# A graph layer's gathers partly replaced by copies of columns: 12 and 14 more columns a step

## The chip, the cores and the metric

The kernel runs on one core of a Trainium2 chip. The metric is the device time of one execution in microseconds. Engines are named PE (TensorE), DVE (VectorE), ACT (ScalarE), POOL (GpSimd) and SP (SyncE, which here issues most transfers).

## The reference

One message-passing layer over a graph of N = 12500 nodes with 64 features and E = 200000 edges, sorted by destination:

```
nodes = x[edges].reshape(E, 128)                      # source row, destination row
gates = (ssp(edge_state @ We1 + be1) @ We2 + be2) * soft_cutoff(distance)
h     = ssp(nodes @ Wn1 + bn1) @ Wn2 + bn2            # ssp(z) = softplus(z) - log 2
sums  = zeros_like(x).at[dst].add(h * gates)
x     = layernorm(x + x + ssp(sums @ Ws1 + bs1) @ Ws2 + bs2)
```

## The kernel before

The edges are cut into 391 groups of 512. A group is four columns (`k` = 0 to 3) of 128 edges. The main loop runs over steps `i`, one group a step, software-pipelined by hand: the program's order on each engine is the order in which the loop writes it (`tc.manual_schedule`).

The source rows of a group reach the chip by four indirect transfers, one for each column, which POOL issues (`gather`, L204); the four of a group follow each other and are called a burst here. They land in `xg`, a tile `[128 edges, 4, 128]` with eight buffers. Its first 64 entries are the source row, the next 42 a one-hot row that says which of 42 neighbouring nodes the edge ends in (`onehot`, L277). TensorE transposes the four columns (`transposes`, L283), ScalarE copies the result out of PSUM (`xcopy`, tile `xT`, L291), and the first layer multiplies it (`layer1_node`, L308) with weights whose lower rows are the destination nodes' own products, read from a table in HBM (SP, `wns`). ScalarE takes exponential and logarithm (`exps` L322, `logs` L325), VectorE finishes the softplus (L330). The second layer (`layer2`, L354 and L359) gives gates and `h`; VectorE multiplies them (`hcut` L368, `message` L372). `scatter` (L376) multiplies the messages with the one-hot rows, and `window` (L396) adds the result to `sums`. Matmuls called `busy` (L334) fill TensorE's idle time.

In step `i` TensorE's order is: the biases, `scatter(i-2)`, `transposes(i+1)`, the edge part of layer 1, a `busy` matmul or, early on, the table's next chunk (`chunk`, L646), `layer1_node(i+1)`, a `busy` matmul, `layer2(i)`. A gather of group `g` reuses the `xg` buffer of group `g-8` and so waits for `scatter(g-8)`.

Every so often a block of 512 nodes has all its edges, and its final part is worked in pieces over the next steps (`node_block`): two of the pieces have matmuls (`hidden` L415, `layer2` L443 and L446), and the others are VectorE's and ScalarE's (L425 to L475).

Some columns of edges are not gathered. Half of x lies transposed on the chip (`xh`, 128 partitions by 6250 columns of 4 bytes; nodes from 6250 on are in the upper 64 partitions). `columns(i, queue, pool)` copies single columns of `xh`, at addresses read into registers, into a tile `column` of 128 columns (L259); queue 0 is VectorE, 8 copies a step, and queue 1 is ScalarE, 16 a step, from step 8 on. `read_columns` loads the addresses into the engine's registers (L242). When 128 columns are whole, `choose` (L271) clears for each edge the half that isn't its node, with the help of a tile `side` that SP loads. The result enters `layer1_node` as one more matmul (L311), and the column of `xg` is set to zero instead of being gathered (L202). Which column of which group this is, a slot, is fixed ahead by `slots_by_columns`: a slot is placed as soon as enough columns have been copied, and never in two adjacent groups. In a step the copies of ScalarE stand behind `xcopy`, and the ones of VectorE behind the softplus and the one-hot rows:

```
xcopy(i + 1)
columns(i, 1, finish)
...
at(onehot, i + 3)
read_columns(i, 0)
columns(i, 0, finish)
choose(finish)
```

Of the kernel before, what the change touches and what calls it, by code (L numbers as in the profile page):

```python
# [12 lines left out]
U8 = mybir.dt.uint8  # L13
# [12 lines left out]
P = 128  # L26
# [8 lines left out]
AHEAD = 3  # L35
# [5 lines left out]
BEHIND = 5  # L41
# [2 lines left out]

BLOCK_STEPS = ((2, 3, 4, 4, 6, 7, 8, 9, 10, 14), (2, 3, 3, 4, 5, 6, 7, 8, 9, 10), (1, 2, 1, 2, 3))
COLUMNS = (8, 16)
BASES = 4
COLUMNS_FROM = 8
XH_PARTS = 4
# [21 lines left out]
    return steps  # L71


def slots_by_columns(NG):

    slots, taken = [], set()
    for queue in (1, 0):
        columns, n = COLUMNS[queue], 0
        for g in range(NG - 2):
            if (g - 3 - COLUMNS_FROM + 1) * columns >= (n + 1) * P and not {g - 1, g, g + 1} & taken:  # L80
                slots.append((queue, g, queue + 1))
                taken.add(g)
                n += 1
    return sorted(slots)


def column_columns(NG):

    queues = [queue for queue, _, _ in slots_by_columns(NG)]
    return [-(-queues.count(queue) // columns) * columns if columns else 0 for queue, columns in enumerate(COLUMNS)]  # L90


def chunk_of(i, NCH):
# [11 lines left out]
def gnn_resnorm_kernel(ctx: ExitStack, tc: tile.TileContext, a: dict, out: bass.AP, E: int):  # L105
    nc = tc.nc
    x = a["x"]
    N = x.shape[0]
    NG = a["eT"].shape[1]
# [55 lines left out]
    be3 = const.tile([PIECES, 2, D], BF16, name="be3")  # L165
    row3 = const.tile([PIECES, 2, K, D], BF16, name="row3")
    rs3 = const.tile([PIECES, K, D], BF16, name="rs3")
    slots = slots_by_columns(NG)
    by_columns = {(g, k) for _, g, k in slots}
    columns_of = column_columns(NG)  # L170
    columns_at = const.tile([P, sum(columns_of)], I32, name="columns_at")
# [56 lines left out]
    engines = ((nc.vector, DVE), (nc.scalar, ACT))  # L228
    own = [[slot for slot in slots if slot[0] == queue] for queue in range(2)]
    column_tiles, side_tiles, chosen_columns = {}, {}, {}  # L230
    column_at, columns_done, whole = [[], []], [0, 0], []

    def columns_left(i, queue):
        return len(own[queue]) * P - columns_done[queue] if i >= COLUMNS_FROM else 0

    def read_columns(i, queue):

        if columns_left(i, queue) <= 0:
            return
        n, count = columns_done[queue], COLUMNS[queue]  # L240
        p, q = (n // count) % P, queue * columns_of[0] + n // (count * P) * count
        column_at[queue] = nc.values_load_multi_w_load_instructions(  # L242
            columns_at[p : p + 1, q : q + count], engines=[engines[queue][1]], min_val=xh_at,
            max_val=xh_at + 4 * (half_n - 1), skip_runtime_bounds_check_because="src holds rows of x")[1]

    def columns(i, queue, pool):

        count = min(COLUMNS[queue], columns_left(i, queue))
        for j in range(count):
            m, r = divmod(columns_done[queue] + j, P)  # L250
            slot = own[queue][m]
            if r == 0:
                column_tiles[slot] = pool.tile([P, P], F32, name=f"column{queue}", bufs=2)
                side_tiles[slot] = pool.tile([P, P], I32, name=f"side{queue}", bufs=2)
                at = slots.index(slot)
                nc.sync.dma_start(side_tiles[slot], a["sides"][at : at + 1, :].rearrange("o p -> (o p)")
                                  .partition_broadcast(P))
            copy = nc.vector.tensor_copy if queue == 0 else nc.scalar.copy
            copy(column_tiles[slot].bitcast(U8)[:, 4 * r : 4 * r + 4], xh[:, bass.ds(column_at[queue][j] - xh_at, 4)])  # L259
            if r == P - 1:  # L260
                whole.append(slot)
        columns_done[queue] += max(count, 0)

    def choose(pool):

        while whole:
            queue, g, k = slot = whole.pop(0)
            chosen_columns[g, k] = pool.tile([P, P], F32, name=f"chosen{queue}", bufs=2)
            for h, op in enumerate((OP.is_lt, OP.is_ge)):
                part = slice(h * D, (h + 1) * D)  # L270
                nc.vector.scalar_tensor_tensor(chosen_columns[g, k][part], side_tiles[slot][part], float(half_n),  # L271
                                               column_tiles[slot][part], op, OP.mult)
# [51 lines left out]
    def logs(g, part=every):  # L324
        nc.scalar.activation(us[g][:, part], us[g][:, part], AF.Ln, bias=one)  # L325
# [160 lines left out]
    with tc.manual_schedule():  # L486
# [50 lines left out]
        def clear(first, last):  # L537
            nc.vector.memset(sums[:, first * P : WIDE if last == NCH else last * P], 0.0)
# [43 lines left out]
        for i, w in enumerate((we2[:D, 0, :], wn2)):  # L582
            n = w.shape[0]
# [83 lines left out]
        with tc.tile_pool(name="finish", bufs=1) as finish:  # L667
# [4 lines left out]
            def at(f, g, *more):  # L672
                if 0 <= g < NG:
                    f(g, *more)
# [13 lines left out]
            for i in range(-1, last - 1):  # L688
                now = parts.pop(i, [])
                early = [part for part in now if part.tensor]  # L690
                at(load, i + LOADS)
                if i >= 0:
                    at(gather, i + AHEAD, range(K), [("transposes", i)] if i < BEHIND else ())
                layer1_bias(i + 1)
                at(layer2_bias, i)
                for n, g in enumerate(behind_by(i)):
                    scatter(g, zs[i + 1][:, 1, HE + 2 * n * W : HE + 2 * (n + 1) * W])
                transposes(i + 1, ("load", i + 1), ("gather", i + 1), ("onehot", i + 1))
                xcopy(i + 1)
                columns(i, 1, finish)  # L700
                layer1_edge(i + 1)
                c = chunk_of(i, NCH)
                if c is None:
                    busy_before_node(i + 1)
                else:
                    beside_sums = zs[i + 1][:, 1, HE + 2 * W : HE + 2 * W + P]
                    chunk(c, beside_sums)
                layer1_node(i + 1)
                exps(i + 1)
                logs(i + 1)  # L710
                if c is not None:
                    keep_chunk(c, beside_sums)
                read_columns(i + 1, 1)
                for g in behind_by(i):
                    window(g)
                if c is not None:
                    clear(c, c + 1)
                at(busy_before_layer2, i)
                at(layer2, i)
                for part in early:  # L720
                    part.tensor(tx_tile())
                at(hcut, i)
                at(message, i)
                softplus(i + 1)
                for part in early:
                    part.others()
                at(onehot, i + 3)
                read_columns(i, 0)
                columns(i, 0, finish)
                choose(finish)  # L730
                for part in now:
                    if not part.tensor:
                        part.others()
                for action in beside.get(i, []):
                    action()
# [134 lines left out]
def layouts(inputs):  # L870
# [8 lines left out]
    NG = -(-E // GE)  # L879
# [3 lines left out]
    def padded(v, n, fill):  # L883
        return np.concatenate([v, np.full((n - v.shape[0],) + v.shape[1:], fill, v.dtype)])
# [8 lines left out]
    slots = slots_by_columns(NG)  # L893
    out["sides"] = np.ascontiguousarray(np.stack([src_slots[:, g, k] for _, g, k in slots]))
    parts = []
    for queue, (count, n) in enumerate(zip(COLUMNS, column_columns(NG))):
        if n:
            v = np.concatenate([src_slots[:, g, k] for q, g, k in slots if q == queue])
            parts.append(padded(v, P * n, 0).reshape(-1, P, count).transpose(1, 0, 2).reshape(P, n))
# [52 lines left out]
```

## Time and profile before

| | us |
|---|---|
| median of 3 runs | 2363.53 (2359.99 to 2370.90) |
| the profiled execution | 2389.88 |
| its span, first to last instruction | 2388.1 |
| PE busy | 1970.5 (83%) |
| PE weight load busy | 1656.7 (69%) |
| ACT busy | 1511.2 (63%) |
| POOL busy | 1417.0 (59%), 1493 gathers |
| DVE busy | 1293.9 (54%) |

A line of the timeline reads: start in us from the start of the span, duration in us, engine, line of the kernel, operation, tile written and tiles read, shapes, how many such instructions are merged, and in brackets the engine's idle time before it and what ended that. A line of the waits reads: engine, tile and line that waited, for what; total in us, how often, the longest. A line such as `L242 ACTq TENSOR_LOAD ... x2: a/b/c, s to t` gives shortest, median and longest duration in ns and the start of the first and the last in us; a q behind the engine says that its sequencer runs it.

### The profile page before, as it was taken

The numbers are of one execution on the slowest core, as the hardware profiler recorded it, in microseconds if no ns is written. First come the engines' busy times: TensorE is split into PE (matmuls) and PEld (weight loads), VectorE is DVE, ScalarE is ACT, GpSimd is POOL, SyncE is SP. The second block draws the span as 40 slices with busy tenths as digits, with TensorE's granted clock in tenths as the row PEclk, the third lists the DMA queues.
The fourth block names the chain that finished last, engine by engine and source line by source line (L and its number), as shares of the span: only waits on it lengthen the run. The fifth ranks groups of instructions, "written<-read, shape, count | busy, mean of one in ns | idle before, by whom it ended". The sixth has DMA issues, their size and how long they took to land.

```text
span 2388.1 us, 48209 instructions
## 1 busy us (share of the span) xinstructions
PE 1970.5 (83%) x12897; PEld 1656.7 (69%) x12897; DVE 1293.9 (54%) x5966; ACT 1511.2 (63%) x7412; POOL 1417.0 (59%) x1497
## 2 busy tenths in 40 slices
PE   6788888888888888888888888888888888888877
PEld 4666677767776776677677667766777767777765
DVE  4355555555555555555555555555555555555544
ACT  3466666666666666666666666666666666666653
POOL 5665665666666666666666666665665666666650
PEclk9799999999999999999999999999999999999988
DMA  6332232322222222222222222222222222222220
GB/s 185 85 91 68 56 75 56 77 61 71 54 57 56 53 59 54 57 56 62 53 59 55 57 58 55 59 59 54 58 58 56 59 57 60 63 57 58 59 50 14
DMA packets 159679, 148.63 MB, mean 62 GB/s; under 512 B 40564, under 2 KB 108949, under 8 KB 159274
## 3 DMA queue, kind: packets, MB, share of 16 engines
q1 hardware_dynamic: 111194, 94.97, 14.4%
q0 software_dynamic: 47776, 49.02, 10.8%
q8 instruction: 109, 1.79, 0.3%
q14 instruction: 166, 1.36, 0.2%
q10 hardware_dynamic: 434, 1.50, 0.2%
HBM read 135.70 MB, written 9.62 MB: 61 GB/s over the span
## 4 chain that ended last, share of the span: by engine, by line
PE 80%; issue 13%; ACT 3%; DVE 2%; another core or an unknown queue 1%; DMA 0%; DVEq 0%; ACTq 0%
PE z L308 18%; PE gh L359 13%; PE z L376 10%; PE tx L283 10%; PE gh L354 7%; PE z L301 6%; PE gh L334 4%; PE gh L347 3%; PE z L296 3%; PE z L334 2%; ACT xT L291 2%; PE tx L415 1%; PE tx L446 1%; PE z L311 1%
## 5 line engine op out<-in xcount | busy, mean ns | idle before, releaser
L204 POOL DMA_INDIRECT xg<-in_x,src_i x1493 | 1416.8, 949 | 919.3 <-PE tx L283 488.8
L308 PE MATMUL z<-xT,wns 106*128 106x256 f32 x1564 | 459.7, 412 | 359.9 <-issue 285.9
L291 ACT COPY xT<-tx 106x512 f32<-106x512 f32 x391 | 229.1, 586 | 779.3 <-PE tx L283 751.1
L259 ACT COPY column<-xh 128x4 uint8 x6016 | 608.7, 193 | 0.0
L308 PEld LDWEIGHTS z<-xT,wns 106*128 106x128 f32 x1564 | 267.8, 193 | 452.4 <-issue 337.7
L368 DVE TENSOR_TENSOR h<-gh,cut 128x256 f32<-128x256 f32 x391 | 165.9, 424 | 747.9 <-PE tx L283 632.2
L359 PE MATMUL gh<-consts,s 128*128 128x64 f32 x3128 | 396.0, 270 | 0.0
L359 PEld LDWEIGHTS gh<-consts,s 128*128 128x128 f32 x3128 | 385.0, 194 | 0.1
L325 ACT ACTIVATE u<-u,one 128x768 f32<-128x768 f32 x392 | 365.8, 933 | 13.4 <-ACT u L322 0.5
L330 DVE SCALAR_TENSOR_TENSOR s<-u,z 128x768 f32<-128x768 f32 x392 | 368.7, 941 | 0.4 <-issue 0.4
L322 ACT ACTIVATE u<-z 128x768 f32<-128x768 f32 x392 | 314.7, 803 | 43.4 <-PE z L308 19.0
L396 DVE TENSOR_TENSOR sums<-sums,z 64x42 f32 x778 | 152.4, 196 | 291.3 <-issue 207.4
L376 PEld LDWEIGHTS z<-xg,msg 128*128 128x128 f32 x1556 | 205.0, 192 | 140.6 <-issue 121.3
L376 PE MATMUL z<-xg,msg 128*128 128x84 f32 x1556 | 265.1, 293 | 15.3 <-DVE msg L372 15.3
L259 DVE COPY column<-xh 128x4 uint8 x2944 | 246.5, 219 | 0.4 <-issue 0.4
L354 PE MATMUL gh<-consts,s 128*128 128x128 f32 x1564 | 243.3, 279 | 1.3 <-DVE s L330 0.8
L283 PE MATMUL tx<-consts,xg 128*106 128x128 f32 x1564 | 238.1, 276 | 0.0
L301 PE MATMUL z<-eT,consts 128*128 128x256 f32 x782 | 237.3, 386 | 0.0
L354 PEld LDWEIGHTS gh<-consts,s 128*128 128x128 f32 x1564 | 210.0, 195 | 2.0 <-DVE s L330 1.1
L283 PEld LDWEIGHTS tx<-consts,xg 128*106 128x106 f32 x1564 | 182.5, 142 | 0.9 <-issue 0.9
L372 DVE TENSOR_TENSOR msg<-gh,h 128x256 f32<-128x256 f32 x391 | 165.8, 424 | 13.4
L334 PEld LDWEIGHTS gh<-consts 128*128 128x128 f32 x778 | 149.5, 195 | 20.5 <-issue 0.3
(109 smaller groups left out, 1456.2 us busy)
## 6 DMA issues: line engine op xcount, KB each, us to landing
eT<-in_eT SPq DMA_DIRECT2D x195, 256.0 KB
xg<-in_x,src_i POOLq DMA_INDIRECT x1493
wns<-table SPq DMA_DIRECT2D x782, 21.0 KB
table<-tb SPq DMA_DIRECT2D x14, 448.0 KB
side<-in_sides SPq DMA_DIRECT2D x70, 64.0 KB
y<-in_x SPq DMA_DIRECT2D x24, 128.0 KB
out<-y SPq DMA_DIRECT2D x24, 128.0 KB
xh<-in_xh SPq DMA_DIRECT2D x2, 781.5 KB
```

The costliest lines, as they stand in the source:

```text
L204: behind(note(("gather", g), nc.gpsimd.indirect_dma_start(out=xg[:, k, :D], out_offset=None, in_=x, in_offset=bass.IndirectOffsetOnAxis(ap ...
L259: copy(column_tiles[slot].bitcast(U8)[:, 4 * r : 4 * r + 4], xh[:, bass.ds(column_at[queue][j] - xh_at, 4)])
L283: ins = nc.tensor.transpose(tx[:, k, :], xgs[g][:, k, :DW], ident)
L301: nc.tensor.matmul(zs[g][:, 0, :HE], we1.rearrange("a h d -> a (h d)"), eTs[g], start=False, stop=True, skip_group_check=True)
L308: nc.tensor.matmul(zn, wns[:, g % REST, h, :], xTs[g][:, h], start=True, stop=not chosen, skip_group_check=True)
L322: nc.scalar.activation(us[g][:, part], z_of(g)[:, part], AF.Exp)
L325: nc.scalar.activation(us[g][:, part], us[g][:, part], AF.Ln, bias=one)
L330: nc.vector.scalar_tensor_tensor(ss[g].rearrange("p i t e -> p (i t e)")[:, part], us[g][:, part], BIG, z_of(g)[:, part], OP.min, OP.max)
L334: nc.tensor.matmul(z, we1.rearrange("a h d -> a (h d)"), ident, start=True, stop=True, skip_group_check=True)
L354: nc.tensor.matmul(v[:, 0, t], ss[g][:, 0, t, :], we2, start=False, stop=False, skip_group_check=True)
L359: nc.tensor.matmul(ghs[g][:, 1, 2 * t + h, :], ss[g][:, 1 + h, t, :], wn2, start=False, stop=h == 1 and t == 1, skip_group_check=True)
L376: ins = nc.tensor.matmul(sc, msgs[g][:, 2 * t : 2 * t + 2, :].rearrange("p h f -> p (h f)"), xgs[g][:, 2 * t : 2 * t + 2, D:DW], start=t = ...
```

## The change

`slots_by_columns` becomes `column_plan`, which also says how many columns each engine copies in each step. Beside the 8 (VectorE) and 16 (ScalarE) of before, `MORE` = 12 and 14 columns are copied in a step `i` where the group `i + FLYING` has no slot, with FLYING = 5 for VectorE and 6 for ScalarE. With more columns there are more slots. `columns` and `read_columns` get a `part`:

- ScalarE: part 0 (16 columns) stays behind `xcopy`; part 1 (14) comes behind the logarithm and the copy of a table chunk. The load of addresses for part 1 stands behind the logarithm, the one for the next step's part 0 behind part 1.
- VectorE: part 0 (12 columns) comes behind `window` and the clearing of sums and ahead of `hcut`; part 1 (the 8 of before) stays in its place. The load for the next step's part 0 stands behind part 1.
- `choose` handles a slot one call later than it was completed.

The array of addresses is laid out anew, with room for 150 columns in place of 72, and more `side` rows are passed. Lines behind the changed ones move by 15 to 18: L204 becomes L222, L242 L257, L259 L274, L271 L289, L283 L301, L291 L309, L311 L329, L368 L386.

```diff
+MORE = (12, 14)
+FLYING = (AHEAD + BEHIND - 3, AHEAD + BEHIND - 2)
...
+def column_plan(NG):
+
+    taken, slots, n = set(), [], [0, 0]
+
+    def more(queue, i, known):
+        g = i + FLYING[queue]
+        return MORE[queue] if COLUMNS_FROM <= i and g <= known and g not in taken else 0
+
+    def count(queue, i, known):
+        return (COLUMNS[queue] if i >= COLUMNS_FROM else 0) + more(queue, i, known)
+
+    for g in range(NG - 2):
+        for queue in (1, 0):
+            if sum(count(queue, i, g - 1) for i in range(g - 3)) >= (n[queue] + 1) * P and not {g - 1, g} & taken:
+                slots.append((queue, g, queue + 1))
+                taken.add(g)
+                n[queue] += 1
...
                 xcopy(i + 1)
-                columns(i, 1, finish)
+                columns(i, 1, 0, finish)
...
                 logs(i + 1)
+                read_columns(i, 1, 1)
                 if c is not None:
                     keep_chunk(c, beside_sums)
-                read_columns(i + 1, 1)
+                columns(i, 1, 1, finish)
+                read_columns(i + 1, 1, 0)
                 for g in behind_by(i):
                     window(g)
                 if c is not None:
                     clear(c, c + 1)
+                columns(i, 0, 0, finish)
                 at(busy_before_layer2, i)
                 at(layer2, i)
...
                 at(onehot, i + 3)
-                read_columns(i, 0)
-                columns(i, 0, finish)
+                read_columns(i, 0, 1)
+                columns(i, 0, 1, finish)
+                read_columns(i + 1, 0, 0)
                 choose(finish)
```

More of the change, by code (lines that the diff above doesn't have):

```diff
@@ L71, in block_steps @@
     return steps
[L74 to L80, printed above, removed]
+def column_plan(NG):
[8 more added lines that the diff above has]
+            if sum(count(queue, i, g - 1) for i in range(g - 3)) >= (n[queue] + 1) * P and not {g - 1, g} & taken:
                 slots.append((queue, g, queue + 1))
                 taken.add(g)
-                n += 1
-    return sorted(slots)
+                n[queue] += 1
+    counts = []
+    for queue in range(2):
+        left, counted = n[queue] * P, []
+        for i in range(NG):
+            sets = (more(queue, i, NG), COLUMNS[queue] if i >= COLUMNS_FROM else 0)
+            counted.append([])
+            for wanted in sets[:: 1 - 2 * queue]:
+                counted[-1].append(min(left, wanted))
+                left -= counted[-1][-1]
+        counts.append(counted)
+    return sorted(slots), counts
 def column_columns(NG):
-    queues = [queue for queue, _, _ in slots_by_columns(NG)]
-    return [-(-queues.count(queue) // columns) * columns if columns else 0 for queue, columns in enumerate(COLUMNS)]
+    return [-(-(NG - COLUMNS_FROM) // P) * (few + more) for few, more in zip(COLUMNS, MORE)]
 def chunk_of(i, NCH):
@@ L167, in gnn_resnorm_kernel @@
     rs3 = const.tile([PIECES, K, D], BF16, name="rs3")
-    slots = slots_by_columns(NG)
+    slots, counts = column_plan(NG)
     by_columns = {(g, k) for _, g, k in slots}
@@ L230, in gnn_resnorm_kernel, with read_columns, columns @@
     column_tiles, side_tiles, chosen_columns = {}, {}, {}
[L231 to L248, printed above, removed]
+    column_at, columns_done, whole, chosen_next = {}, [0, 0], [], []
+    def read_columns(i, queue, part):
+        count = counts[queue][i][part] if 0 <= i < NG else 0
+        if count:
+            row, block = (i - COLUMNS_FROM) % P, (i - COLUMNS_FROM) // P
+            first = queue * columns_of[0] + block * (COLUMNS[queue] + MORE[queue]) + part * counts[queue][i][0]
+            column_at[queue, part] = nc.values_load_multi_w_load_instructions(
+                columns_at[row : row + 1, first : first + count], engines=[engines[queue][1]], min_val=xh_at,
+                max_val=xh_at + 4 * (half_n - 1), skip_runtime_bounds_check_because="src holds rows of x")[1]
+    def columns(i, queue, part, pool):
+        count = counts[queue][i][part] if 0 <= i < NG else 0
         for j in range(count):
@@ L258, in columns @@
             copy = nc.vector.tensor_copy if queue == 0 else nc.scalar.copy
-            copy(column_tiles[slot].bitcast(U8)[:, 4 * r : 4 * r + 4], xh[:, bass.ds(column_at[queue][j] - xh_at, 4)])
+            copy(column_tiles[slot].bitcast(U8)[:, 4 * r : 4 * r + 4], xh[:, bass.ds(column_at[queue, part][j] - xh_at, 4)])
             if r == P - 1:
                 whole.append(slot)
-        columns_done[queue] += max(count, 0)
+        columns_done[queue] += count
     def choose(pool):
-        while whole:
-            queue, g, k = slot = whole.pop(0)
+        ready = list(chosen_next)
+        chosen_next[:] = whole
+        del whole[:]
+        for slot in ready:
+            queue, g, k = slot
             chosen_columns[g, k] = pool.tile([P, P], F32, name=f"chosen{queue}", bufs=2)
@@ L892, in layouts @@
     src_slots = out["src_l"].reshape(P, NG, K)
-    slots = slots_by_columns(NG)
+    slots, counts = column_plan(NG)
     out["sides"] = np.ascontiguousarray(np.stack([src_slots[:, g, k] for _, g, k in slots]))
     parts = []
[L896 to L899, printed above, removed]
+    for queue, n in enumerate(column_columns(NG)):
+        v = np.concatenate([src_slots[:, g, k] for q, g, k in slots if q == queue])
+        part, done = np.zeros((P, n), v.dtype), 0
+        for i, count in enumerate(map(sum, counts[queue])):
+            if count:
+                block, row = divmod(i - COLUMNS_FROM, P)
+                part[row, block * (COLUMNS[queue] + MORE[queue]) :][:count] = v[done : done + count]
+                done += count
+        parts.append(part)
     out["columns"] = np.ascontiguousarray(np.concatenate(parts, axis=1))
```

## The prediction

> **What bounds the kernel now.** I read first the list of waits, then a stretch of the timeline. A "step" below is the time from one `xT` copy of ScalarE (L291) to the next, step i from `xcopy(i+1)` to `xcopy(i+2)`; there are 391 of these copies. A "burst" is the row of gathers of one group that POOL issues.
>
> ```profile
> ACT xT L291 <- PE tx L283: 751.1, 375, 12.0
> DVE h L368 <- PE tx L283: 632.2, 279, 2.8
> POOL xg L204 <- PE tx L283: 488.8, 342, 7.2
> ```
>
> Three engines wait for TensorE's transposes, nearly every step. The timeline shows that the transposes are not what is late:
>
> ```profile
> 1203.52 0.59 ACT L291 COPY xT<-tx 106x512 f32<-106x512 f32 x1 [1.73 <-PE tx L283]
> 1203.69 0.94 POOL L204 DMA_INDIRECT xg<-in_x,src_i  x1 [1.41 <-PE tx L283]
> 1204.00 1.62 ACT L259 COPY column<-xh 128x4 uint8 x16
> 1204.94 0.95 POOL L204 DMA_INDIRECT xg<-in_x,src_i  x1 [0.30 <-issue]
> 1205.29 0.66 DVE L259 COPY column<-xh 128x4 uint8 x8
> 1206.36 0.93 ACT L325 ACTIVATE u<-u,one 128x768 f32<-128x768 f32 x1
> 1206.36 0.41 DVE L396 TENSOR_TENSOR sums<-sums,z 64x42 f32 x2 [0.41 <-issue]
> 1207.44 0.94 POOL L204 DMA_INDIRECT xg<-in_x,src_i  x1 [0.30 <-issue]
> 1207.66 0.60 PE L283 MATMUL tx<-consts,xg 128*106 128x128 f32 x4
> 1209.56 0.42 DVE L368 TENSOR_TENSOR h<-gh,cut 128x256 f32<-128x256 f32 x1 [2.79 <-PE tx L283]
> 1209.69 0.59 ACT L291 COPY xT<-tx 106x512 f32<-106x512 f32 x1 [2.40 <-PE tx L283]
> 1212.37 0.94 POOL L204 DMA_INDIRECT xg<-in_x,src_i  x1 [0.30 <-issue]
> 1213.84 0.60 PE L283 MATMUL tx<-consts,xg 128*106 128x128 f32 x4
> 1214.35 0.42 DVE L368 TENSOR_TENSOR h<-gh,cut 128x256 f32<-128x256 f32 x1 [1.41 <-PE z L376]
> 1214.48 0.59 ACT L291 COPY xT<-tx 106x512 f32<-106x512 f32 x1 [0.28 <-PE tx L283]
> 1220.69 0.59 ACT L291 COPY xT<-tx 106x512 f32<-106x512 f32 x1 [2.43 <-PE tx L283]
> ```
>
> In the first step the burst has four gathers. The transposes end at 1207.66 + 0.60 = 1208.26, yet the `xT` copy starts at 1209.69, 1.43 us later, and so do `h` and the next burst; the last gather ended at 1207.44 + 0.94 = 1208.38, and everything moves 1.2 to 1.3 us after that. In the second step the burst has three (the last ends at 1213.31): `xT` starts at 1214.48, 0.04 us behind the transposes' end. So TensorE's completions reach nobody until about 1.1 us behind a burst's last gather. A step with four gathers ("long") is bound by the burst: 6.17 us here and 6.21 us in the next. A step with three ("short") takes 4.79 us and is bound by TensorE and the `xT` copy. Why the completions are held I leave open; the sum needs only the two prices. For the long price I take 6.13 us, from four long steps in a row (24.49 / 4 = 6.12) and the longer two above:
>
> ```profile
> 1260.89 0.59 ACT L291 COPY xT<-tx 106x512 f32<-106x512 f32 x1 [1.01 <-PE tx L283]
> 1285.38 0.59 ACT L291 COPY xT<-tx 106x512 f32<-106x512 f32 x1 [2.37 <-PE tx L283]
> ```
>
> **The change, part by part.** A slot (group, column) built by copies takes one gather from its group's burst. Worked out from the two plans for 391 groups, there are 70 slots before (23 by VectorE, 47 by ScalarE) and 121 after (47 and 74), never two in adjacent groups. The pool of `xg` has eight buffers, and `scatter(i-2)` stands in step i, so the burst inside step i is that of group i+6. Of the 369 steps from 8 to 376, 69 are short before and 119 after.
>
> *Gain.* A short step saves 6.13 - 4.79 = 1.34 us, less what TensorE does in it beyond the usual. Rows for that: the matmul of a slot (L311), and short steps with the node block's first (L415) or second matmuls (L446).
>
> ```profile
> 1239.07 0.22 PE z L311 x2
> 654.74 0.59 ACT L291 COPY xT<-tx 106x512 f32<-106x512 f32 x1 [2.31 <-PE tx L283]
> 660.40 0.59 ACT L291 COPY xT<-tx 106x512 f32<-106x512 f32 x1 [1.89 <-PE tx L283]
> 1350.15 0.59 ACT L291 COPY xT<-tx 106x512 f32<-106x512 f32 x1 [2.31 <-PE tx L283]
> 1356.09 0.59 ACT L291 COPY xT<-tx 106x512 f32<-106x512 f32 x1 [2.16 <-PE tx L283]
> ```
>
> With L446 a short step takes 5.66 us (saves 0.47), with L415 5.94 us (saves 0.19), with L311 4.79 + 0.22 = 5.01 us (saves 1.12). Before: 62 plain, 4 with L446, 3 with L415, none with L311, since no two slots lie five groups apart there: 83.1 + 1.9 + 0.6 = 85.6 us saved. That this model holds: 62 x 4.79 + 4 x 5.66 + 3 x 5.94 + 300 x 6.13 = 2176 us, and these 369 steps took 2281.65 - 97.47 = 2184 us.
>
> ```profile
> 97.47 0.59 ACT L291 COPY xT<-tx 106x512 f32<-106x512 f32 x1 [2.30 <-PE tx L283]
> 2281.65 0.59 ACT L291 COPY xT<-tx 106x512 f32<-106x512 f32 x1 [2.33 <-PE tx L283]
> ```
>
> After, slots often lie five apart: 66 plain (88.4), 39 with L311 alone (43.7), 6 with L446 (2.8), 8 with L415 (1.5), less 3 x 0.22 where L311 comes on top: 135.7 us. The gain is 50 us.
>
> *ScalarE's 14 copies and second load* stand in all 250 long steps and in no short one. ScalarE's own rows:
>
> ```profile
> L242 ACTq TENSOR_LOAD <-columns_at x2: 1051/1054/1057, 1200.3 to 1206.4; - x2
> L242 DVEq TENSOR_LOAD <-columns_at x2: 611/614/617, 1204.0 to 1210.2; - x2
> L322 ACTq EVENT_SEMAPHORE  x1: 17/17/17, 1210.7 to 1210.7; - x1
> ```
>
> Loads cost 0.055 us a register between 8 (0.61) and 16 (1.05), so 14 take 0.94. The load starts with the logarithm (both at 1206.4), as today's does, and is hidden by it (0.93 us). Sixteen copies in 1.62 us are 0.095 us apart, so 14 take 1.43. The next load must wait until the copies are handed over, not until they are done: the exponential's semaphore comes at 1210.7, 1.0 us after the `xT` copy at 1209.69, while the 16 copies ran until 2.1 us after their own. That is 0.06 us a copy. Counted from the step's `xT` copy: logarithm to 3.77, copies handed over by 4.66 and done by 5.30, second load (16 registers, 1.05) done by 5.72. The next `xT` copy is due at 6.17, so 0.45 us is left and the addition costs nothing by itself. If that cover is gone (the load waits for the last copy), it ends at 6.36, 0.19 us late. ScalarE's node work stands behind the second load and loses its cover:
>
> ```profile
> 1270.95 0.42 ACT L434 ACTIVATE l_s<-l_s 128x256 f32<-128x256 f32 x1 [0.17 <-issue]
> 1271.40 0.51 ACT L435 ACTIVATE l_s<-l_s,half 128x256 f32<-128x256 f32 x1
> 1273.12 0.59 ACT L291 COPY xT<-tx 106x512 f32<-106x512 f32 x1 [1.22 <-PE tx L283]
> ```
>
> Its start moves from 3.95 (1270.95 less `xT` at 1267.00, 6.12 before 1273.12) to about 5.74, and only 1.22 us were free: 0.57 us late. A late `xT` copy in front of a long step is absorbed, since the burst was released without it and TensorE has 1.43 us to spare; in front of a short step it is paid. That is 7 steps with logarithms, some 5 with the two short activations at half of that: 5.5 us.
>
> *VectorE's 12 copies* take 0.66 + 4 x 0.071 = 0.94 us behind the sums and ahead of `h`, where VectorE idles 2.79 us in a long step and 1.41 in a short one; their load (about 0.83) runs beside the eight copies and the wait for `sums`. The plan asks whether group i+5 has a slot, while the burst in flight is i+6, so these copies stand in all 119 short steps and in 131 long ones. In the short ones 0.47 us is left. Node work of up to 1.2 us then makes `h` late; the following step is always long and absorbs it. Cost 1 us, bounds 0 and 119 x 0.47 = 56 us (all cover gone and nothing absorbed).
>
> *The 51 extra choices* on VectorE lie in idle time, but slow a gather beside them:
>
> ```profile
> 2277.88 1.20 DVE L271 SCALAR_TENSOR_TENSOR chosen<-side,column 64x128 f32<-64x128 int32 x4
> 2278.22 1.06 POOL L204 DMA_INDIRECT xg<-in_x,src_i  x1 [0.31 <-issue]
> ```
>
> That is 0.12 us, mattering in long steps and not for every choice: 2 us (bounds 0 and 6). The 51 extra `side` loads on SP, the clearing memsets, the wider `columns` array and the deferral of a choice by one step lie off the path: 0.5 us for the prologue's wider operations.
>
> *Weighing a rule.* The Trainium skill, SBUF — State Buffer, section "SBUF: two separate sides", says that VectorE and GpSimd share a port pair, that a VectorE copy inside SBUF can take it for its whole length, and that GpSimd then cannot write the gathers' descriptors. The trace does not bear that out here: the gather at 1204.94, with eight such copies at 1205.29, took 0.95 us, and the one before it, 0.94.
>
> *Sum.* 50 - 5.5 - 1 - 2 - 0.5 = 41 us. The profiled execution took 2389.9 us, so its like would take 2349; the median of the runs, 2363.5, lies 26 lower, and I carry the difference over: 2322 us.
>
> **The rivals.**
>
> *ScalarE becomes the bound (slower).* Place: behind the 14 copies of a long step. If the second load starts only when the copies are done, or takes longer than 1.05 us, the next `xT` copy is late; at 0.19 us late 250 steps lose 48 us and the time is 2370, at 0.45 late 113 us and 2435. It decides at 0.17 us a step (41 / 250). I take 2390. For it: only 0.45 us is left by an estimate of the hand-over rate. Against: the semaphore row at 1210.7, and that TensorE's 1.43 us absorbs some. Chance 0.13.
>
> *Short steps lengthen.* The 12 copies fall into every short step, against the change's own words; if `h` is late there and layer 2 behind it isn't absorbed, up to 56 us go: 2350 at half of it. Against: every short step is followed by a long one. Chance 0.11.
>
> *VectorE's copies hold the gathers.* With 0.12 us a burst, as beside a choice, 131 long steps lose 16 us: 2338; with the whole 0.94 us, 123 us: 2445. The rule quoted above would give the second; the gather of 0.95 us speaks against both. Chance 0.03.
>
> *Nothing moves*, because a gather less isn't what makes a step short: 2363. The 4.79 against 6.17 speaks against it. Chance 0.02.
>
> **How the numbers follow.** My forecast has 0.71. Its own range is 2300 (costs at zero, L311 hidden: 50 x 1.34 = 67 us) to 2340. The range 2297 to 2360 adds the second rival and most of the third. Half a per cent, about 12 us, is what a measurement of this kernel tells from no change. Faster: 0.71 + 0.07 + 0.02 = 0.80; same: 0.05; slower: 0.15, the first rival with the bad ends of the others.
>
> **What would show it.** Right: 1442 gathers; steps of 4.8 to 5.0 us where the burst has three and of 6.1 where it has four; idle time before `xT` in long steps down from 2.4 to about 0.9 us, still ended by the transposes; idle before `h` in short steps down from 1.4 to about 0.5. Wrong: `xT` that follows ScalarE's own work with no idle time, long steps over 6.2 us, short ones over 5.1 us without extra matmuls, gathers of over 1 us beside columns.

## The result, and the profile after

The changed kernel takes 2853.77 us (median of 4 runs, 2850.31 to 2876.76), the kernel before 2366.28 beside it: a ratio of 1.208 (95% interval 1.201 to 1.215). The prediction was 2322. The profiled execution took 2850.31 us, its span 2848.5.

The loss has a place. Three windows of the changed kernel (length, then busy time and instructions of PE, PE's weight loads, DVE, ACT and POOL, then TensorE's granted clock, the DMA engines' busy share and GB/s):

```profile
100.00:860.00 760.00, 664.54 (x4172) 549.49 (x4172) 510.62 (x3056) 624.15 (x3722) 443.24 (x468) 0.96 0.28 65
860.00:2030.00 1170.00, 830.88 (x4037) 700.09 (x4036) 490.70 (x2906) 595.57 (x3501) 426.18 (x448) 0.75 0.16 36
2030.00:2700.00 670.00, 574.98 (x3733) 482.49 (x3732) 458.69 (x2688) 546.53 (x3228) 389.62 (x409) 0.97 0.26 59
```

The middle window does as little as the 760 us ahead of it (448 gathers against 468) in 1170 us, and every engine is busy for a smaller share of it. But for its first 7 us it lies in the second block of 128 steps, 136 to 263. The `xT` copies that bound these steps, in the timeline:

```profile
866.83 0.59 ACT L309 COPY xT<-tx 106x512 f32<-106x512 f32 x1 [2.58 <-issue]
...
2096.43 0.59 ACT L309 COPY xT<-tx 106x512 f32<-106x512 f32 x1 [1.20 <-PE tx L301]
```

That is 1229.6 us, where the kernel before took 1609.34 - 855.40 = 753.9:

```profile
855.40 0.59 ACT L291 COPY xT<-tx 106x512 f32<-106x512 f32 x1 [2.34 <-PE tx L283]
...
1609.34 0.59 ACT L291 COPY xT<-tx 106x512 f32<-106x512 f32 x1 [2.35 <-PE tx L283]
```

475.7 us more; the two medians of the runs differ by 487. In the other two thirds, medians are 6.13 and 6.07 us for a long step and 5.01 for a short one, as forecast; in the middle they are 10.56 and 7.62. One slow step, ScalarE's part of the timeline:

```profile
1200.42 0.59 ACT L309 COPY xT<-tx 106x512 f32<-106x512 f32 x1 [2.40 <-issue]
1200.90 1.63 ACT L274 COPY column<-xh 128x4 uint8 x16
1202.43 0.81 ACT L340 ACTIVATE u<-z 128x768 f32<-128x768 f32 x1
1203.27 0.94 ACT L343 ACTIVATE u<-u,one 128x768 f32<-128x768 f32 x1
1206.38 1.44 ACT L274 COPY column<-xh 128x4 uint8 x14 [2.18 <-issue]
1210.26 0.59 ACT L309 COPY xT<-tx 106x512 f32<-106x512 f32 x1 [2.43 <-issue]
```

ScalarE stands still twice, 2.18 us ahead of the 14 copies and 2.43 us ahead of the next `xT`, and both times for "issue": for nothing but its own sequencer. The sequencer's loads of addresses in the first and the second window (shortest, median and longest in ns; sizes mixed):

```profile
L257 ACTq TENSOR_LOAD <-columns_at x213: 1007/1054/2110, 102.3 to 856.7; - x107
...
L257 ACTq TENSOR_LOAD <-columns_at x205: 1272/3477/3754, 861.5 to 2029.5; - x103
L257 DVEq TENSOR_LOAD <-columns_at x206: 594/622/1073, 859.3 to 2029.6; - x103
```

By size and block of 128 steps, medians worked out from all load rows: ScalarE's 16 take 1.04 us in the first and third block and 3.56 in the second, its 14 take 1.25 and 3.06; VectorE's 8 and 12 take 0.61 and 0.86 in every block. The waits that grew, over the whole run:

```profile
ACT column L274 <- issue: 244.9, 230, 2.3
...
ACT xT L309 <- issue: 205.3, 93, 2.8
```

Together they are 450 us, 387 of them in the second block; before, the first did not occur and the second (for L291) was 2.3 us. For TensorE ScalarE waited 149 us in that block (ahead of `xT` and of the exponential), less than the 251 us in the same steps of the kernel before.

### The profile page after: what moved, and what is told of

Same layout as the page of the kernel before. It is cut to its first block, busy times and chain, and to the rows that moved or that the text cites. A ratio compares the mean times of both kernels' runs of the same rounds, so it can differ in the third digit from the quotient of the medians.

```text
span 2848.5 us, 55570 instructions
## 1 busy us (share of the span) xinstructions
PE 2253.2 (79%) x12999; PEld 1881.7 (66%) x12999; DVE 1588.1 (56%) x9191; ACT 1881.5 (66%) x10868; POOL 1372.5 (48%) x1446
## 4 chain that ended last, share of the span: by engine, by line
PE 39%; ACT 34%; issue 13%; ACTq 8%; DVE 4%; DMA 1%; another core or an unknown queue 1%; DVEq 1%; SPq 0%
ACT column L274 16%; PE z L326 11%; ACTq L257 8%; PE gh L377 7%; ACT u L343 6%; ACT u L340 5%; ACT xT L309 5%; PE z L394 5%; PE tx L301 4%; PE gh L372 4%; PE gh L352 2%; PE gh L365 2%; PE z L314 1%; PE z L319 1%; DVE column L274 1%
## 5 line engine op out<-in xcount | busy, mean ns | idle before, releaser
L222 POOL DMA_INDIRECT xg<-in_x,src_i x1442 | 1372.3, 952 | 1424.2 <-PE z L394 342.9
L274 ACT COPY column<-xh 128x4 uint8 x9472 | 974.2, 195 | 246.9 <-issue 244.9
L326 PE MATMUL z<-xT,wns 106*128 106x256 f32 x1564 | 535.4, 464 | 530.6 <-ACT xT L309 364.3
L326 PEld LDWEIGHTS z<-xT,wns 106*128 106x128 f32 x1564 | 304.5, 221 | 628.3 <-ACT xT L309 410.5
L309 ACT COPY xT<-tx 106x512 f32<-106x512 f32 x391 | 228.3, 584 | 483.5 <-PE tx L301 237.1
L274 DVE COPY column<-xh 128x4 uint8 x6016 | 506.1, 190 | 4.7 <-issue 0.5
L377 PE MATMUL gh<-consts,s 128*128 128x64 f32 x3128 | 447.5, 293 | 0.0
L377 PEld LDWEIGHTS gh<-consts,s 128*128 128x128 f32 x3128 | 442.5, 218 | 0.1
L386 DVE TENSOR_TENSOR h<-gh,cut 128x256 f32<-128x256 f32 x391 | 166.1, 425 | 315.4 <-PE tx L301 187.6
L394 PE MATMUL z<-xg,msg 128*128 128x84 f32 x1556 | 287.1, 311 | 9.0 <-DVE msg L390 7.0
L372 PE MATMUL gh<-consts,s 128*128 128x128 f32 x1564 | 285.3, 313 | 10.4 <-DVE s L348 7.3
L372 PEld LDWEIGHTS gh<-consts,s 128*128 128x128 f32 x1564 | 247.0, 225 | 18.4 <-DVE s L348 12.5
L301 PE MATMUL tx<-consts,xg 128*106 128x128 f32 x1564 | 258.7, 292 | 0.0
L301 PEld LDWEIGHTS tx<-consts,xg 128*106 128x106 f32 x1564 | 200.4, 153 | 0.9 <-issue 0.9
L352 PE MATMUL gh<-consts 128*128 128x128 f32 x778 | 174.5, 310 | 3.8 <-DVE msg L390 1.6
```

The source lines that it names most:

```text
L222: behind(note(("gather", g), nc.gpsimd.indirect_dma_start(out=xg[:, k, :D], out_offset=None, in_=x, in_offset=bass.IndirectOffsetOnAxis(ap ...
L301: ins = nc.tensor.transpose(tx[:, k, :], xgs[g][:, k, :DW], ident)
L309: note(("xcopy", g), nc.scalar.copy(xT, xTs[g]))
L326: nc.tensor.matmul(zn, wns[:, g % REST, h, :], xTs[g][:, h], start=True, stop=not chosen, skip_group_check=True)
L352: nc.tensor.matmul(z, we1.rearrange("a h d -> a (h d)"), ident, start=True, stop=True, skip_group_check=True)
L372: nc.tensor.matmul(v[:, 0, t], ss[g][:, 0, t, :], we2, start=False, stop=False, skip_group_check=True)
```

## The experiments

There were five sets of runs, each on a chip of its own, with the kernel before beside it: that took 2367 us in the first set, 2395 in the second, and 1995 in the last three, of which more below. Ratios are within a set.

**Is it where the addresses lie?** ScalarE's addresses begin at column 60 and each block of 128 steps had 30 columns more. A column has 4 bytes, so blocks 0, 1 and 2 begin at 240, 360 and 480 bytes: a multiple of 16, 8 beyond one, a multiple. VectorE's sets of 12 and 8 all begin on a multiple. Theory A: a load that begins on a multiple of 16 bytes fetches four registers at a time, any other one by one. Theory B: something else slows the middle steps, such as the amount of work or the clock.

First, the same kernel with 32 columns to a block:

```diff
+PITCH = tuple(-(-(few + more) // 4) * 4 for few, more in zip(COLUMNS, MORE))
...
-            first = queue * columns_of[0] + block * (COLUMNS[queue] + MORE[queue]) + part * counts[queue][i][0]
+            first = queue * columns_of[0] + block * PITCH[queue] + part * counts[queue][i][0]
```

> The changed kernel with one difference: the blocks of 30 addresses that ScalarE loads are laid 32 apart, so that each block begins at a multiple of 16 bytes (in the changed kernel the second block begins at 90 x 4 = 360 bytes, 8 past such a multiple). Theory A, the place of the addresses: a load that begins at a multiple of 16 bytes fetches four registers at once, any other one each by itself (0.217 us a fetch); then all of ScalarE's loads take 1.04 us (16) and 1.25 us (14), as they did in steps 8 to 135 and from 264 on, and at that stretch's medians (short 5.1, long 6.1) 119 x 5.1 + 250 x 6.1 = 2132 us in place of the 2184 of before: about 2314 us. Theory B, the time: something else in steps 136 to 263 (the granted clock of 0.75, other traffic) slows the loads; then they take 3.0 and 3.5 us there again, and the time stays at about 2850 us. Theory C, that the change is slow by what ScalarE has to do, the loads' place apart: over 2400 us.

Measured: 2358.75 us, ratio 0.996 (0.995 to 0.997). The 20% is gone; the loads of the middle window and three waits, in that kernel:

```profile
L258 ACTq TENSOR_LOAD <-columns_at x340: 998/1052/1571, 859.6 to 2029.6; - x170
```

```profile
ACT column L275 <- issue: 98.8, 271, 0.7
...
ACT tb L668 <- issue: 22.0, 55, 0.7
...
ACT xT L310 <- issue: 8.0, 15, 1.5
```

TensorE's granted clock is 0.99 in that window again. But the gain is 8 us instead of some 50; that is taken up below. Second, the changed kernel with two columns ahead of ScalarE's addresses, which puts blocks 0 and 2 off the multiple and block 1 on it:

```diff
-    return [-(-(NG - COLUMNS_FROM) // P) * (few + more) for few, more in zip(COLUMNS, MORE)]
+    return [-(-(NG - COLUMNS_FROM) // P) * (few + more) + gap for few, more, gap in zip(COLUMNS, MORE, (2, 0))]
```

> The changed kernel with ScalarE's addresses moved by two columns (8 bytes): now the first and third blocks begin 8 bytes past a multiple of 16, and the second at one. Theory A (place): the slow loads of 3.0 and 3.5 us move to steps 8 to 135 and 264 to 390, and steps 136 to 263 become fast; the slow third cost about 540 us, or 4.2 us a step, so 241 slow steps make about 3330 us. Theory B (time): the loads of steps 136 to 263 stay slow and the others fast, about 2850 us.

Measured: 3292.21 us in one execution. Now steps 136 to 263 are the quick ones: by the `xT` copies at 93.91, 1350.19 and 2089.42 us they take 739.2 us, and the 128 steps ahead of them 1256.3. Third and fourth, the kernel before, with two empty columns ahead of ScalarE's addresses, and with VectorE's moved by one column and ScalarE's by four:

```diff
+GAPS = (0, 2)     # the fourth run: (1, 3)
...
-        p, q = (n // count) % P, queue * columns_of[0] + n // (count * P) * count
+        p, q = (n // count) % P, GAPS[0] + queue * (columns_of[0] + GAPS[1]) + n // (count * P) * count
```

> The kernel before, with a gap of two columns (8 bytes) ahead of ScalarE's addresses and nothing else: all of ScalarE's loads of 16 begin 8 bytes past a multiple of 16. Theory A: each takes about 3.5 us in place of 1.05; it begins 2.84 us after the xT copy and so ends at 6.3, which makes long steps 6.4 in place of 6.13 and short ones 6.4 in place of 4.79: about 2560 us, more if TensorE's clock falls. Theory B: loads of 1.05 us and 2366 us.

Measured: 2732.85 us in one execution. Two empty columns cost the old kernel 15%. That is more than the 2560 expected: plain steps take 6.5 us, near the 6.4 forecast, but 118 steps take over half a us longer than that, many of them with node work or table chunks, which the estimate had left out. The loads from 860 to 2030 us:

```profile
L243 ACTq TENSOR_LOAD <-columns_at x172: 3409/3566/3767, 862.0 to 2023.3; - x172
L243 DVEq TENSOR_LOAD <-columns_at x172: 593/611/847, 863.1 to 2025.6; - x172
```

> The kernel before, with VectorE's addresses moved by one column (4 bytes) and ScalarE's by four (16 bytes): a measurement of the loads themselves. Theory A: VectorE's loads of 8 take 8 x 0.217 + 0.17 = 1.9 us in place of 0.61, ScalarE's stay at 1.05; VectorE's idle time ahead of h covers the 1.3 us more, so 2366 to 2385 us. If only places 8 bytes off are slow, or only ScalarE's loads: 0.61 us and 2366 us.

Measured: 2383.0 us in one execution. VectorE's loads tripled, and ScalarE's, four columns (16 bytes) further, did not change:

```profile
L243 DVEq TENSOR_LOAD <-columns_at x199: 1841/1901/2264, 861.5 to 2022.1; - x199
L243 ACTq TENSOR_LOAD <-columns_at x199: 1001/1040/1291, 863.8 to 2028.4; - x199
```

So it is the address, on either engine; B falls. Starts 4 and 8 bytes beyond a multiple of 16 were run, 12 was not. One formula fits: 0.18 us and 0.215 us a fetch, with a fetch of four registers where the load begins on a multiple of 16 bytes and of one for the rest or otherwise. 8, 12 and 16 aligned are 2, 3 and 4 fetches (0.61, 0.83, 1.04; measured 0.61, 0.86, 1.04). 14 aligned are 3 + 2 (1.26; measured 1.25). 8 and 16 unaligned come to 1.90 and 3.62 (measured 1.90, and 3.48 to 3.57), 14 to 3.19 (3.06). That it fetches so is inferred from the durations.

**Where the gain of the aligned kernel goes.** Theory S: ScalarE gives it back. In the kernel with a pitch of 32, 107 of 250 long steps have an `xT` copy that follows ScalarE's own work (an operation or a load of addresses) within 0.12 us; against the later of the transposes' end and 1.2 us behind the last gather they are late by 25.7 us in all, 15.0 of it in steps 8 to 70. Such a step of that kernel:

```profile
198.90 0.94 ACT L344 ACTIVATE u<-u,one 128x768 f32<-128x768 f32 x1
...
200.23 0.27 ACT L668 COPY tb<-z 128x128 f32<-128x128 f32 x1 [0.40 <-issue]
...
200.39 0.95 ACT L275 COPY column<-xh 128x4 uint8 x9
...
201.12 0.60 PE L302 MATMUL tx<-consts,xg 128*106 128x128 f32 x4
...
201.52 0.57 ACT L275 COPY column<-xh 128x4 uint8 x5 [0.18 <-issue]
...
202.64 0.59 ACT L310 COPY xT<-tx 106x512 f32<-106x512 f32 x1 [0.55 <-issue]
```

The load of 14 outlasts the logarithm by 0.40 us, the copy of a table chunk (91 of them, in steps 0 to 90) waits behind it and the 14 behind that. The second load starts only at 201.54, by its own row, and takes its usual 1.04 us, so `xT` starts 0.92 us behind the transposes' end. Theory V: VectorE's copies in short steps make `h` late. VectorE's part alone (`MORE = (12, 0)`), ScalarE's alone (`MORE = (0, 14)`), VectorE's copies moved into the long steps, and both from step 91 on, all with aligned sets:

```diff
-FLYING = (AHEAD + BEHIND - 3, AHEAD + BEHIND - 2)
+FLYING = (AHEAD + BEHIND - 2, AHEAD + BEHIND - 2)     # VectorE in long steps
...
+MORE_FROM = 91     # from step 91, with this line and the next two
...
-        return MORE[queue] if COLUMNS_FROM <= i and g <= known and g not in taken else 0
+        return MORE[queue] if MORE_FROM <= i and g <= known and g not in taken else 0
```

> VectorE's 12 copies alone (every set of addresses on a 16-byte multiple): 96 slots and 94 short steps instead of 69. Theory S (what eats the gain is ScalarE: its loads and 14 copies run into its other work, and in the run with a pitch of 32 columns 107 long steps have an xT copy that follows ScalarE's own work without a pause, 25.7 us late together): ScalarE's work is that of before here, so the 25 short steps bring about 29 us and the time is 2335 to 2345 us, short steps 4.79 and long ones 6.1. Theory V (the 12 copies in short steps make h and layer 2 late): the time stays at 2355 to 2370 us, and plain short steps take more than 4.9 us.

> ScalarE's 14 copies alone (every set of addresses on a 16-byte multiple): 100 slots and 98 short steps. Theory S: the 29 short steps and the extra matmuls are worth some 27 us, and ScalarE gives nearly all of it back: 2355 to 2370 us, with the late xT copies as in the run with both parts. Theory V: about 2340 us, the gain is kept.

> The changed kernel with a pitch of 32 columns, and VectorE's 12 copies asked for group i+6, so that they stand in all 250 long steps and in no short one; slots and gathers are the same 121 and 1442. Theory S: no change against the run with a pitch of 32 alone, 2355 to 2363 us. Theory V: faster than it by 15 us or more, below 2345 us.

> The changed kernel with a pitch of 32 columns, and the second sets of both engines only from step 91, behind the stage in which ScalarE also copies the chunks of the table (92 copies, the last in step 90): 110 slots, 108 short steps. Theory S: the 11 short steps lost cost 13 us, and the table's stage, steps 8 to 90, takes about 486 us as before instead of 496: time 2345 to 2356 us, a little below the run with a pitch of 32 alone (2359). If the table's stage has no part in it: 2368 to 2373 us.

Measured, beside a kernel before of 2395.4 us: VectorE alone 2377.35, ratio 0.994 (0.992 to 0.996); ScalarE alone 2403.28, 1.004 (1.002 to 1.006); VectorE in long steps 2392.66, 1.000 (0.998 to 1.002); from step 91 2376.55, 0.994 (0.992 to 0.996). VectorE's copies bring more than they cost; ScalarE's part alone is a loss; moving VectorE's copies out of the short steps brings nothing, and with VectorE's part alone plain short steps stay at 4.79 us. V falls. VectorE's part alone was expected to bring 29 us and brought 15 (0.62% of 2395), so S is not all. The table's stage, steps 8 to 90, from the `xT` copies at its ends, first with VectorE in long steps and then with both from step 91:

```profile
95.15 0.59 ACT L310 COPY xT<-tx 106x512 f32<-106x512 f32 x1 [2.28 <-PE tx L302]
...
608.68 0.59 ACT L310 COPY xT<-tx 106x512 f32<-106x512 f32 x1
```

```profile
93.03 0.59 ACT L311 COPY xT<-tx 106x512 f32<-106x512 f32 x1 [2.28 <-PE tx L303]
...
585.70 0.59 ACT L311 COPY xT<-tx 106x512 f32<-106x512 f32 x1 [2.18 <-PE tx L303]
```

513.5 us against 492.7, though the first has more short steps there. What S lacks is in the long steps' price. The time from a burst's last gather to the next burst is 1.44 us in the first profile of the kernel before (median of the long steps), and in the kernel from step 91 it is 1.44 in steps 8 to 70 and 1.51 from 91 on; with either part alone 1.46 to 1.48, with VectorE's copies in all long steps 1.53 to 1.54. Put together, for these four on one chip (us):

| kernel | gain by the prediction's prices | late `xT` | longer gap x long steps | sum | measured |
|---|---|---|---|---|---|
| VectorE alone | 26 | 0 | 0.03 x 275 = 8 | 18 | 15 |
| ScalarE alone | 26 | 31 | 0.035 x 271 = 9 | -14 | -10 |
| VectorE in long steps | 50 | 36 | 0.09 x 250 = 22 | -8 | 0 |
| both from step 91 | 36 | 18 | 0.07 x 193 = 14 | 4 | 15 |

The measured column is 2395.4 times one less the ratio. The order is right and no sum is off by more than 11 us. In the first set the gap of the kernel with a pitch of 32 is 1.43 us, which beside 1.44 would be no growth at all. But the only profile there with the copies of before, the fourth run above, has a gap of 1.36 us and long steps of 6.06; on that base it is 0.07 x 250 = 18, and 50 - 26 - 18 = 6 us against 8 measured. VectorE's loads are slow in that run, so the base is not a clean one. That the gap grows is seen in one run, from step 91 on; why it grows with the copies is open.

**Sizes of ScalarE's second set, and sets of runs in which nothing waits behind a burst.** To see whether a smaller second set of ScalarE's keeps its gain, it was cut to 8 and to 12 and begun at step 91, VectorE's kept from step 8; VectorE alone got 16; and the kernel before ran again for a profile.

```diff
-MORE = (12, 14)
+MORE = (12, 8)     # and (12, 12), (16, 0)
+MORE_FROM = (8, 91)
...
-        return MORE[queue] if COLUMNS_FROM <= i and g <= known and g not in taken else 0
+        return MORE[queue] if MORE_FROM[queue] <= i and g <= known and g not in taken else 0
```

> VectorE's 12 copies from step 8 as in the changed kernel, ScalarE's second set cut to 8 (a load of two fetches, 0.61 us, and 0.8 us of copies) and begun at step 91, all sets on 16-byte multiples: 107 slots, 105 short steps. Theory S (ScalarE's second set is too long for what is left of its step): with 8 it fits, no xT copy is late, and the 36 added short steps bring what VectorE's 25 brought in proportion: 0.62% x 36/25, a ratio of 0.991. If a second set of any size costs about what it brings: 0.994, as with VectorE's part alone.

> The same with 12 copies by ScalarE (a load of three fetches, 0.85 us, 1.2 us of copies): 113 slots, 111 short steps. Theory S: some xT copies late again, more than with 8 and fewer than with 14: ratio 0.989 to 0.993. If the length of the set doesn't matter: 0.9895, by 42 added short steps in proportion.

> VectorE's part alone with 16 copies instead of 12 (1.2 us, a load of 1.05): 104 slots, 102 short steps. If the copies still fit in front of h in short steps (0.47 us was worked out as left behind 12): 0.62% x 33/25, a ratio of 0.992. If they make h late there: 0.994 or more, plain short steps over 4.9 us.

> The kernel before once more, for a profile on the chip that runs the others. If the time by which the next burst follows the last gather is a property of the chip, it is 1.44 us here as in the first profile; if the added copies and loads lengthen it, it is shorter here than in the kernels beside it.

Measured: the kernel before takes 1994.95 us (1999.42 in the execution with the profile). ScalarE's 8 take 2067.62 (1.037, 1.034 to 1.040), its 12 2117.07 (1.061, 1.059 to 1.063), and VectorE's 16 alone 2107.0 (1.056, 1.054 to 1.058). The unchanged kernel's profile there, timeline of two steps with POOL and ScalarE, then the chain:

```profile
1012.77 0.95 POOL L204 DMA_INDIRECT xg<-in_x,src_i  x1 [0.30 <-issue]
...
1013.37 0.60 PE L283 MATMUL tx<-consts,xg 128*106 128x128 f32 x4
...
1014.01 0.59 ACT L291 COPY xT<-tx 106x512 f32<-106x512 f32 x1 [1.01 <-PE tx L283]
1014.02 0.94 POOL L204 DMA_INDIRECT xg<-in_x,src_i  x1 [0.30 <-PE tx L283]
...
1015.27 0.94 POOL L204 DMA_INDIRECT xg<-in_x,src_i  x1 [0.30 <-issue]
...
1018.79 0.59 ACT L291 COPY xT<-tx 106x512 f32<-106x512 f32 x1 [1.01 <-PE tx L283]
```

```profile
PE 92%; ACT 4%; DVE 1%; DMA 1%; issue 1%; ACTq 0%; POOL 0%; DVEq 0%; POOLq 0%
```

The gathers take the same 0.94 us, but `xT` starts 0.04 us behind the transposes' end (1013.97), whatever POOL does, and the next burst 0.30 us behind the last gather, not 1.44 us as in the first profile. The median long step is 4.78 us, the same as a short one, and 92% of the chain is TensorE. Nothing is held behind a burst (the hold, from here on), so a gather less saves nothing, and each slot costs its matmul (0.22 us) and its copies. Two more sets took up the sizes again:

> VectorE's part alone again, as the measure for the next two on one chip. Where a long step of the kernel before takes 6.1 us: ratio 0.994 as before. Where it takes 4.8 (completions not held): the 12 copies in 94 short and 181 long steps lie in front of h, the gain is nil, ratio 1.01 to 1.03.

> ScalarE's second set of 8 from step 91 beside VectorE's 12. Where long steps take 6.1 us, theory S (the set of 14 is too long): no late xT copies, ratio 0.991; if any second set costs what it brings: 0.994. Where they take 4.8: 1.037 as measured on such a chip.

> ScalarE's second set of 12 from step 91 beside VectorE's 12. Where long steps take 6.1 us, theory S: 0.989 to 0.993, some late xT copies; if any second set costs what it brings: 0.994. Where they take 4.8: 1.061 as measured on such a chip.

> The changed kernel with a pitch of 32 columns, both second sets from step 8. Where long steps take 6.1 us: 0.996 as before. Where they take 4.8 (TensorE 98% busy in the kernel before): the second set of 14 stands in front of xT in all long steps and delays it more than with 12: ratio 1.07 to 1.10.

Measured: 1996.3 us before; VectorE alone 1.023 (1.020 to 1.025), with ScalarE's 8 1.036 (1.034 to 1.039), with its 12 1.060 (1.058 to 1.063), the pitch of 32 with 14 1.120 (1.117 to 1.122), above the 1.07 to 1.10 expected. What VectorE's part alone loses, it loses early: steps 8 to 90 take 453.7 us against 418.6 before, steps 91 to 376 only 13 us more. There VectorE's `sums` wait for ScalarE's copy of the table chunk, the 12 copies stand behind that and ahead of `h`, and layer 2 waits for the softplus 41 times (2 before); that this chain is the price was read from the waits and not tested. Without the hold one sees what ScalarE needs for a long step, in the kernel with a pitch of 32:

```profile
1099.42 0.57 ACT L310 COPY xT<-tx 106x512 f32<-106x512 f32 x1
1099.89 1.62 ACT L275 COPY column<-xh 128x4 uint8 x16
1101.41 0.80 ACT L341 ACTIVATE u<-z 128x768 f32<-128x768 f32 x1
1102.24 0.93 ACT L344 ACTIVATE u<-u,one 128x768 f32<-128x768 f32 x1
1103.59 1.43 ACT L275 COPY column<-xh 128x4 uint8 x14 [0.41 <-issue]
1105.03 0.59 ACT L310 COPY xT<-tx 106x512 f32<-106x512 f32 x1
```

5.61 us, with no pause but the 0.41 us by which the load of 14 outlasts the logarithm. From step 91 on the median long step is 5.11 with 12 and 5.01 with 8.

> Where long steps of the kernel before take 6.1 us, theory S: no late xT copies, ratio 0.991; if any second set of ScalarE's costs what it brings: 0.994. Where they take 4.8: 1.036 as twice before.

> Where long steps take 6.1 us, theory S: 0.989 to 0.993, some late xT copies; if any second set costs what it brings: 0.994. Where they take 4.8: 1.060 as twice before.

Measured: 1.036 (1.033 to 1.039) and 1.060 (1.056 to 1.063), again beside a kernel before of 1995 us. What the sizes bring where completions are held stays open. There the best versions measured are VectorE's part alone and both parts from step 91, each 0.994; where they are not held, the kernel before is the fastest one measured.

## Why the prediction was wrong

*The step that failed* is the price of ScalarE's loads, under "ScalarE's 14 copies and second load". "Loads cost 0.055 us a register between 8 (0.61) and 16 (1.05), so 14 take 0.94" drew a line through two sizes of one alignment. The load of 14 takes 1.25 us where it begins on a multiple of 16 bytes, and 3.06 us in the second block; the second load, taken at 1.05, takes 3.56 there. In that block ScalarE's chain makes the step shown 9.84 us long: the 0.45 us left are gone, and 3.7 us beyond the 6.13. The edit that did it had been read and set aside: "the wider `columns` array" stands among the things off the path for 0.5 us. Its block went from 16 to 30 columns, and that moved the addresses.

*The first rival* was this mechanism at this place: the second load takes longer than 1.05 us, the next `xT` copy is late. Its price of 0.19 to 0.45 us a step was of the wrong size, and its chance of 0.13 rested on the same: it, too, knew loads of one alignment only.

*The gain* of 50 us had the steps' prices right where the hold exists: short steps of 4.79 and 5.01 us and long ones of 6.1 in the two good thirds, with 1442 gathers. Of it, 8 us were left with the loads aligned. And the hold is not the kernel's: in the last three sets the unchanged kernel runs without it, and there is nothing to gain. Each chip was used in one set, so whether it is the chip or something else that differed between the sets was not shown. That rival, "nothing moves, because a gather less isn't what makes a step short", had 0.02.

*ScalarE's slack.* The idle time before `xT` in long steps was to fall to 0.9 us; in the two good thirds the median is 0.06. The estimate that the second load is done 5.72 us behind `xT` is near the 5.61 in which ScalarE gets through a long step above, so in a plain one it still fits; but the copy of the table's chunk, which stands between the logarithm and the 14 copies up to step 90, was not in the sum at all, and node work had 5.5. In the aligned kernel the late `xT` copies come to 25.7 us, 15.0 of them in steps 8 to 70, where the table is copied.

*VectorE's copies* cost no step: the plain short step is 4.79 us with VectorE's part alone, though the median idle time before `h` in short steps fell to 0.29 us there, and to 0.06 with both parts aligned, and not to 0.5. So the second rival fell where the hold exists. The third did, too: in the changed kernel the mean gather is 952 ns against 949, and the 532 gathers that overlap VectorE's copies for over 0.1 us take 951. The Trainium skill, SBUF — State Buffer, section "SBUF: two separate sides", says that a VectorE operation which takes both ports, as an fp32 copy inside SBUF does, keeps GpSimd from writing its descriptors. For these copies of 128x4 uint8, twice as many as before, the 951 ns show nothing of it.

*The sum's base.* The long step's price was taken as a constant, 6.13 us. It rises by 0.03 to 0.09 us with the added copies, some 8 to 22 us over the run. The 6.13 itself came from a profile 26 us above the median of the runs; in the first set's profile with the copies of before it is 6.06.

## What to carry to other kernels

When an edit changes the layout of a small array that an engine's sequencer reads into registers, work out the byte address of every load, block by block, and look up the load's duration for that alignment; pad blocks to 16 bytes. A price fitted to two sizes holds for what the two have in common, here the alignment, and a stage that runs only in part of the steps (the table's chunks) needs its own sum. And before a gain is built on a wait whose cause is open, profile the unchanged kernel on more than one chip.

## What was not expected of the hardware

- A load of 16 registers into ScalarE takes 1.04 us from a multiple of 16 bytes and 3.56 us from 8 bytes beyond one; a load of 8 into VectorE takes 0.61 us, and 1.90 from 4 bytes beyond.
- In some sets of runs ScalarE, VectorE and POOL go on from TensorE's finished transposes only 1.2 to 1.4 us behind a burst of indirect transfers, in others at once; the same kernel takes 2363 to 2395 us in the first and 1995 in the others, at granted clocks of 0.98 and 0.99. What sets it was not found.
- TensorE's granted clock fell to 0.75 in the slow third, where it waited for ScalarE. Its part in the loss was not measured by itself; with the loads aligned it is 0.99 in the same window, and ScalarE's waits for TensorE in the slow third are shorter than before (149 us against 251).
